# A Householder step with one matmul for both of its row products and one for its update, layer 0's work cut into finer pieces beside it

## The chip, the cores and the metric

The kernel runs on one NeuronCore of one Trainium2 chip. The metric is the device time of one execution in microseconds (us), as the median of several runs. The profile is that of one execution, taken by the hardware profiler.

## The reference, cut to what matters

A stack of four graph layers works on `x` of 128 x 64 x 256 (batch, nodes, features) with one adjacency matrix of 64 x 64. Each layer normalises its input over the features, applies a ReLU, and adds its result to `x`.

```python
h = relu(layernorm(x)); x = x + L0(h, adj)   # A_hat mix, Linear 256->512, batchnorm, relu, Linear 512->256, batchnorm
h = relu(layernorm(x)); x = x + L1(h, adj)   # below
h = relu(layernorm(x)); x = x + L2(h, adj)   # two mixes with Linear, then LSTMs over windows of 1 to 4 nodes
h = relu(layernorm(x)); x = x + L3(h, adj)   # attention over 512 edges

def L1(features, A, W1, b1, W2, b2):
    deg = sum(A, axis=0) + sum(A, axis=1) - diagonal(A)
    d = where(deg > 0, rsqrt(deg), 0)
    L_norm = d[:, None] * (diag(deg) - A) * d[None, :]
    _, U = eigh(L_norm)
    agg = einsum('mn,bnd->bmd', U.T, features)
    return einsum('nm,bmd->bnd', U, relu(agg @ W1 + b1) @ W2 + b2)
```

All is float32. Layer 1 needs the eigenvectors `U` of a symmetric 64 x 64 matrix, which depends on `adj` alone. Layer 0 does not need them.

## The kernel before, in words

The engines are TensorE (PE), VectorE (DVE), ScalarE (ACT), GpSimd (POOL) and SyncE (SP, which issues the DMAs). A TensorE instruction loads a stationary operand ("weights", LDWEIGHTS) and streams a moving one through it (MATMUL); a float32 matmul shows in the trace as two passes, so two of each.

The method `eigenvectors` runs first. It puts two kinds of work on the same engines:

- The eigenvector computation of the class `Fast`: `tridiagonal` turns the matrix into a tridiagonal one in 62 Householder steps (`householder`, for c = 63 down to 2). Then `vectors` finds eigenvalues and vectors and ends in a verdict, a count of failures. Its matmuls write PSUM tiles called `fps` and `fvps`.
- Layer 0. `hidden0` walks over 16 blocks of 512 rows of `x` (tiles `X`): for each one, `hidden_block` normalises, mixes the nodes by a block-diagonal matrix `BDH` and multiplies by the first Linear's weights into four PSUM banks `ps`; ACT copies each bank and DVE takes its batchnorm statistics. When all blocks are through, `features0` applies batchnorm and ReLU and multiplies by the second Linear's weights. Before its first product stand 28 matmuls that only keep TensorE running while the statistics are finished. A product here is `ps<-z,w`.

A planner written out by hand (`Plan`) sets the order. A `chain` step is placed on its engine as soon as what it needs is ready. A `beside` step waits in the engine's queue, as filler: ahead of each chain step, `fill` takes filler that would be done before the chain step can start, or late by no more than the engine's slack. The planner reckons with a busy time and a time until ready for each step, both given in the code.

```python
plan = Plan(dict(T=0.6, S=0.3, V=0.3), 5)      # slack in us: T TensorE, S ScalarE, V VectorE; 5 PSUM banks
...
if at is not None and (at + x.busy <= until + self.slack[engine] or x.urgent and at <= until):
```

After `tridiagonal`, `plan.emit()` emits all planned steps in order of their planned time, and TensorE, VectorE and ScalarE keep that order. `vectors` and what is left of layer 0 (`plan.rest()`) are then emitted in turn and interleaved by the framework's own scheduler. A branch on the verdict follows ("holds"), with a slower eigenvector method for the case of failures, then layers 1 to 3.

One Householder step works on the symmetric matrix `A`, its c-th row `x` copied onto 64 partitions, and these operations:

- TensorE: `zp`, the row c-1 of A on c partitions (a column of the identity as weights), and `yp`, the row c of A likewise; both come from A as it stands after the last update.
- ACT: `s0`, the root of the row's square sum; a copy of one element to `OA`; `z`, the copy of `zp` out of PSUM.
- DVE, on one element in each partition: half the sign (`q`), 1/s0 (`r`), `tt`, `nb` = q tt, the corrected elements of `x`, and `KAP`, the reciprocal.
- DVE: `uA` = z nb + yp. ACT: `uk` = KAP x, and SP stores the row `x` in `V` for later.
- DVE: `c2`, the sum over uA uk / 2 (tile `junk`), then `v` = x c2 - uA.
- TensorE: the update, `uk` times `v` plus `v` times `uk`, two matmuls with one row each that accumulate in one PSUM tile. DVE adds it to A.
- DVE: the next row x in two operations from `uk`, `v` and `z`, without waiting for the update of A. ACT: its square sum (tile `ja`).

All operations of TensorE, DVE and ACT go through a recording helper, so the trace gives them one line, L799 (L800 in the changed kernel); tiles tell them apart.

Of the kernel before, what the change touches and what calls it, by code (L numbers as in the profile page):

```python
# [8 lines left out]
F32 = mybir.dt.float32  # L9
I32 = mybir.dt.int32  # L10
AF = mybir.ActivationFunctionType
ALU = mybir.AluOpType
# [772 lines left out]
GRID = 64  # L785

# [56 lines left out]
class Plan:  # L843
# [55 lines left out]

    def rest(self):  # L900

        while any(self.queue.values()):
            for e in self.queue:
                self.fill(e, 1e9)
# [8 lines left out]
class Fast:  # L913
# [31 lines left out]
    def sum(self, out, a, s, b, op0, op1=ALU.mult, name="junk"):  # L945

        w = a.shape[-1]
        j = self.t(f"{name}{a.shape[0]}", a.shape[0], 64)
        self.o.stt(j[:, 0:w], a, s, b, op0, op1, acc=out)
# [3 lines left out]
    def constants(self):  # L953
# [6 lines left out]
        self.P = t("P", 64, 1)  # L960
        iota(self.P[:], [[0, 1]], 0, 1)
# [21 lines left out]
        o.ts(self.low[:], self.J[:64, :], self.P[:], ALU.is_lt)  # L983
# [3 lines left out]
        o.copy(pi[:], self.P[:])  # L987
# [15 lines left out]
    def tridiagonal(self, S, made, plan):  # L1003
# [3 lines left out]
        A = self.A = t("A", 64, 64)  # L1007
# [3 lines left out]
        for x in (KAP, NB, V):  # L1011
            nc.vector.memset(x[:], 0.0)
        s0, r, tt, q, c2 = (t("h_" + x, 64, 1) for x in "s0 r t q c2".split())
        ja = t("ja", 64, 64)
        bc = lambda c, n=64: c.to_broadcast([n, 64])
        now = {}
        go = plan.chain

        def keep(name, a, b):
            now[name] = self.mm((a, b))  # L1020

        d = go("T", lambda: keep("p", S, self.JR[:]), [made], 0.3, 0.5)
        d = go("V", lambda: o.copy(m[:], now["p"][:]), [d], 0.15, 0.28)
        d = go("T", lambda: keep("p", self.JR[:], m[:]), [d], 0.3, 0.5)
        rest = go("V", lambda: o.copy(A[:], now["p"][:]), [d], 0.15, 0.28)
        d = go("T", lambda: keep("p", bc(ident[:64, 63:64]), A[:]), [rest], 0.3, 0.5)

        def first():
            x = now["x"] = self.rows.tile([64, 65], F32, name="f_x", bufs=8)
            o.copy(x[:, 0:63], now["p"][:, 0:63])  # L1030

        def square(w):
            x = now["x"]
            self.act(ja[:, 0:w], x[:, 0:w], AF.Square, accum_out=x[:, w:w + 1])

        row = go("V", first, [d], 0.15, 0.28)
        h = go("S", lambda: square(63), [row], 0.34, 0.42)
        for c in range(63, 1, -1):
            row, h, rest = self.householder(c, now, go, row, h, rest, (s0, r, tt, q, c2), square)

    def householder(self, c, now, go, row, h, rest, scalars, square):

        o, nc, t = self.o, self.nc, self.t
        ident = self.k.ident
        A, NB, OA, KAP, V = self.A, t("NB", 64, 64), t("OA", 64, 64, 2), t("KAP", 64, 64), t("V", 64, 64)
        s0, r, tt, q, c2 = scalars
        bc = lambda a, n=64: a.to_broadcast([n, 64])
        x = lambda a, b: now["x"][:, a:b]
        nb = NB[:, c - 1:c]
        e, w = 0.001 * c, c - 1  # L1050

        def zy():
            now["zp"] = self.ps.tile([64, 64], F32, name="fps")
            nc.tensor.matmul(now["zp"][:, 0:c], bc(ident[0:c, c - 1:c], c), A[0:c, 0:c], start=True, stop=True)
            now["yp"] = self.ps.tile([64, 64], F32, name="fps")
            nc.tensor.matmul(now["yp"][:, 0:c], bc(A[0:c, c:c + 1], c), A[0:c, 0:c], start=True, stop=True)

        def row_z():
            now["z"] = self.rows.tile([64, 64], F32, name="f_z")
            self.act(now["z"][:, 0:c], now["zp"][:, 0:c], AF.Copy)  # L1060

        def row_uk():

            nc.sync.dma_start(V[c:c + 1, 0:c], now["x"][0:1, 0:c])
            now["uk"] = self.rows.tile([64, 64], F32, name="f_uk")
            self.act(now["uk"][:, 0:c], x(0, c), AF.Copy, scale=KAP[:, c:c + 1])

        def row_uA():
            now["uA"] = self.rows.tile([64, 64], F32, name="f_uA")
            o.stt(now["uA"][:, 0:c], now["z"][:, 0:c], nb, now["yp"][:, 0:c], ALU.mult, ALU.add)  # L1070

        def row_v():
            now["v"] = self.rows.tile([64, 64], F32, name="f_v")
            o.stt(now["v"][:, 0:c], x(0, c), c2[:], now["uA"][:, 0:c], ALU.mult, ALU.subtract)

        def outer():
            uk, v = now["uk"], now["v"]
            p = now["p"] = self.ps.tile([64, 64], F32, name="fps")
            nc.tensor.matmul(p[0:c, 0:c], uk[0:1, 0:c], v[0:1, 0:c], start=True, stop=False)
            nc.tensor.matmul(p[0:c, 0:c], v[0:1, 0:c], uk[0:1, 0:c], start=False, stop=True)  # L1080

        def row_x():
            now["x"] = self.rows.tile([64, 65], F32, name="f_x", bufs=8)
            o.stt(x(0, w), now["uk"][:, 0:w], now["v"][:, w:c], now["z"][:, 0:w], ALU.mult, ALU.add)


        z = go("T", zy, [rest], 0.34, 0.42)
        sq = go("S", lambda: self.act(s0[:], x(c, c + 1), AF.Sqrt), [h], 0.13, 0.23)
        oa = go("S", lambda: self.act(OA[:, c, 1:2], x(c - 1, c), AF.Copy), [row], 0.12, 0.22)
        zs = go("S", row_z, [z], 0.15, 0.26 + e)  # L1090
        sg = go("V", lambda: o.ts(q[:], x(c - 1, c), **halve(0)), [row])
        d = go("V", lambda: o.recip(r[:], s0[:]), [sq])
        d = go("V", lambda: o.stt(tt[:], r[:], x(c, c + 1), s0[:], ALU.mult, ALU.add), [d, h])
        b = go("V", lambda: o.mul(nb, q[:], tt[:]), [d, sg])
        d = go("V", lambda: o.stt(x(c - 1, c + 1), OA[:, c, :], nb, x(c - 1, c + 1), ALU.mult, ALU.add), [b, oa])
        d = go("V", lambda: o.recip(KAP[:, c:c + 1], x(c, c + 1)), [d])
        uk = go("S", row_uk, [d], 0.16, 0.32 + e)
        d = go("V", row_uA, [zs, b, z], 0.12 + e, 0.25 + e)
        d = go("V", lambda: self.sum(c2[:], now["uA"][:, 0:c], 0.5, now["uk"][:, 0:c], ALU.mult), [uk, d],
               0.2 + e, 0.28 + e)  # L1100
        v = go("V", row_v, [d], 0.15 + e, 0.26 + e)
        p = go("T", outer, [v], 0.25, 0.45)
        if c > 2:
            row = go("V", row_x, [v], 0.15 + e, 0.22 + e)
            row = go("V", lambda: o.stt(x(0, w), now["v"][:, 0:w], now["uk"][:, w:c], x(0, w), ALU.mult, ALU.add),
                     [row], 0.15 + e, 0.25 + e)
            h = go("S", lambda: square(w), [row], 0.28 + e, 0.36 + e)
        rest = go("V", lambda: o.add(A[0:c, 0:c], A[0:c, 0:c], now["p"][0:c, 0:c]), [p], 0.12 + e, 0.22 + e)
        return row, h, rest

    def reflectors(self):
# [8 lines left out]
        self.sum(kc[:], self.KAPs[:], 1.0, ident, ALU.mult)  # L1120
# [22 lines left out]
    def scale(self):  # L1143

        o, nc, t = self.o, self.nc, self.t
        NB, A = t("NB", 64, 64), self.A
        self.KAPs = t("KAP", 64, 64)
        DM, NE = t("DM", 64, 64), t("NE", 64, 64)
        o.mul(DM[:], A[:], self.k.ident[:64, :64])
# [316 lines left out]
class Kernel:  # L1466
# [340 lines left out]
    def hidden_block(self, i, r, m, plan, needs, used):  # L1807
# [9 lines left out]
        def mix(dc):  # L1817
            p = now["m", dc] = psum.tile([P, BT], F32, name="ps")
            for j in range(TPB):
                self.mm(p[:, j * P:(j + 1) * P], now["h"][:, j, dc * P:(dc + 1) * P], self.BDH[:])  # L1820
# [966 lines left out]
```

## Time and profile before

| | us |
|---|---|
| median of 3 runs | 2329.3 |
| lowest and highest run | 2326.33, 2331.57 |
| profiled execution: span from first to last instruction | 2325.1 |
| profiled execution: its own time around the span | not recorded apart; the span lies 1.2 under the lowest run |
| start until the first Householder matmul | 11.7 |
| Householder with layer 0 beside it, until its last outer product | 272.1 |
| the rest of the eigenvector work with layer 0, until the verdict's matmul | 364.6 |
| branch | to about 378 |
| layers 1 to 3 | to the end |
| mean granted TensorE clock | 0.997 of full speed |

The span is what the profile can explain; the times of the runs are what a change is judged by. The chain that ended last is followed back from the last instruction; the waits of an engine tell whom it waited for; the timeline gives single instructions with start and duration. The weights for the first product arrive early (the first product starts at 22.5), the first mix runs at 17.3, and layer 0's last product ends at about 364.3, with the verdict's matmul right behind it.

### The profile page before, as it was taken

The page shows a single profiled execution, that of the slowest core. Times are in us where ns is not written, and L with a number is a line of the kernel's source. Part 1 is how long each engine was busy: PE and PEld are TensorE (multiplying, and loading weights), DVE is VectorE, ACT ScalarE, POOL GpSimd, SP SyncE. Part 2 cuts the span into 40 slices and gives each one's busy share as a digit, 9 for nine tenths or more (in the row PEclk, how much of TensorE's full clock was granted, in tenths as well). Part 3 has the DMA queues.
Part 4 walks back from the last instruction along what each step waited for, and adds up shares of the span by engine and source line. Part 5 has one row for each costly group of instructions (what it writes and reads, how often), then busy time and mean ns, then how long its engine had stood idle before and what let it go on. Part 6 is the DMA issues. An engine that isn't in the chain of part 4 may idle for free.

```text
span 2325.1 us, 32725 instructions
## 1 busy us (share of the span) xinstructions
PE 2283.6 (98%) x12169; PEld 1633.1 (70%) x12169; DVE 1629.3 (70%) x4054; ACT 1139.5 (49%) x2483; POOL 3.0 (0%) x26
## 2 busy tenths in 40 slices
PE   7999998999999999999999999999999999999999
PEld 4554445676777788888999998888885544554544
DVE  8887676888447777666767676559756686766667
ACT  5765865754436654433444444336435544444321
POOL 0000000000000000000000000000000000000000
PEclk9999999999999999999999999999999999999999
DMA  5000211230000000001000002000010000000001
GB/s 171 1 1 26 65 56 30 71 83 19 1 37 0 1 19 1 1 1 37 1 1 1 1 1 73 1 1 17 1 46 28 1 5 15 15 19 14 14 24 46
DMA packets 61065, 54.81 MB, mean 24 GB/s; under 512 B 15203, under 2 KB 58724, under 8 KB 60900
## 3 DMA queue, kind: packets, MB, share of 16 engines
q1 hardware_dynamic: 60900, 52.66, 7.4%
q8 instruction: 97, 1.59, 0.3%
q14 instruction: 68, 0.56, 0.1%
HBM read 35.86 MB, written 16.78 MB: 23 GB/s over the span
## 4 chain that ended last, share of the span: by engine, by line
PE 79%; DVE 3%; issue 1%; ACT 1%; DMA 0%; SPq 0%; ACTq 0%; DVEq 0%
PE ps L799 69%; PE acc L799 5%; PE pt L799 4%; PE pe L799 1%; PE y L799 1%; DVE aw L799 1%; DVE X L799 1%; DVE sm_m L799 0%; DVE XV L799 0%; ACT ls_g L799 0%; ACT h L799 0%; DVE ls_g L799 0%; ACT big L799 0%; DVE ls_t L799 0%; DVE sm_e L799 0%
## 5 line engine op out<-in xcount | busy, mean ns | idle before, releaser
L799 ACT ACTIVATE ls_g<-ls_g,ls_b 128x512 f32<-128x512 f32 (+4 forms) x472 | 243.1, 565 | 151.4 <-DVE ls_g L799 149.6
L799 ACT ACTIVATE ls_g<-ps,ls_b 128x256 f32<-128x256 f32 (+3 forms) x268 | 115.5, 470 | 330.9 <-PE ps L799 327.7
L799 PE MATMUL ps<-z,w 128*128 128x512 f32 x512 | 254.9, 621 | 0.9 <-ACT z L799 0.9
L799 PE MATMUL ps<-big,X 128*128 128x176 f32 (+3 forms) x848 | 212.7, 366 | 0.1
L799 DVE TENSOR_TENSOR ls_g<-ls_z,ps 128x512 f32<-128x512 f32 (+5 forms) x256 | 146.8, 579 | 91.9 <-PE ps L799 90.4
L799 DVE TENSOR_TENSOR aw<-at,ed_OST 128x1024 f32<-128x1024 f32 x128 | 149.9, 1219 | 83.0 <-PE ps L799 82.8
L799 PE MATMUL ps<-ls_tx,X 128*128 128x160 f32 (+2 forms) x960 | 206.8, 326 | 0.6 <-ACT ls_g L799 0.6
L799 PE MATMUL ps<-X,X 128*128 128x160 f32 (+1 forms) x896 | 199.1, 306 | 0.0
L799 PE MATMUL ps<-X,ls_w 128*128 128x256 f32 x640 | 190.5, 379 | 0.0
L799 PEld LDWEIGHTS ps<-ls_tx,X 128*128 128x128 f32 x960 | 161.8, 190 | 15.1 <-DVE X L799 4.8
L799 PEld LDWEIGHTS ps<-big,X 128*128 128x128 f32 x848 | 145.9, 190 | 29.7 <-issue 19.4
L799 DVE TENSOR_TENSOR X<-ls_g 128x1024 f32<-128x1024 f32 (+2 forms) x108 | 117.4, 1087 | 49.9 <-ACT ls_g L799 49.8
L799 ACT ACTIVATE r<-ps 128x512 f32<-128x512 f32 x256 | 131.6, 614 | 41.5 <-PE ps L799 41.4
L799 PEld LDWEIGHTS ps<-X,X 128*128 128x128 f32 x896 | 148.4, 190 | 0.0
L799 PE MATMUL ps<-X,ls_s 128*128 128x256 f32 x480 | 142.3, 379 | 0.0
L799 PEld LDWEIGHTS ps<-z,w 128*128 128x128 f32 x512 | 87.2, 190 | 69.0 <-issue 60.2
L799 PE MATMUL ps<-ls_tx,ls_s 128*128 128x256 f32 x464 | 134.8, 379 | 0.0
L799 PE MATMUL ps<-ed_S,Q 64*128 64x512 f32 x512 | 132.9, 618 | 1.4 <-DVE hT L799 0.7
L799 PE MATMUL ps<-ls_tx,ls_w 128*128 128x256 f32 x464 | 133.2, 380 | 0.0
L799 PEld LDWEIGHTS ps<-X,ls_w 128*128 128x128 f32 x640 | 121.4, 190 | 16.8 <-DVE X L799 0.3
L799 PE MATMUL ps<-big,ls_w 128*128 128x256 f32 x464 | 131.9, 379 | 0.7 <-ACT ls_z L799 0.7
L799 PE MATMUL ps<-aw,ed_ODT 128*64 128x512 f32 x512 | 117.3, 595 | 0.1
(545 smaller groups left out, 4019.0 us busy)
## 6 DMA issues: line engine op xcount, KB each, us to landing
X<-in_x_dram SPq DMA_DIRECT2D x32, 512.0 KB
xs<-X SPq DMA_DIRECT2D x16, 512.0 KB
X<-xs SPq DMA_DIRECT2D x16, 512.0 KB
out_dram<-X SPq DMA_DIRECT2D x31, 256.0 KB
X<-in_L_gnn_Wih_t_dram SPq DMA_DIRECT2D x4, 512.0 KB
ls_w<-in_L_gnn_Wih_t_dram SPq DMA_DIRECT2D x4, 512.0 KB
ls_w<-in_L_gnn_Whh_t_dram SPq DMA_DIRECT2D x4, 512.0 KB
w<-in_L_gnn_W_t_dram SPq DMA_DIRECT2D x2, 512.0 KB
```

The source lines that it names most:

```text
L799: i = method(*a, **kw)
```

## The change

- z and y come from one matmul. Its weights `EX` have 128 columns: one half is a unit vector c-1 in each column, written by ACT (`unit`, two steps ahead); the other is the column c of A, masked to its rows, written by DVE (`m`) from the PSUM tile of the update, ahead of the add to A.
- The update is one matmul of "uneven" operands `L` (left) and `R` (right) with 65 rows: rows 0 to 63 of `R` are `v`, of `L` they are zero but for row 0; row 64 of both holds the other vectors. ACT writes the single rows (`side`): minus uA into row 64 of `L`, KAP x into row 0 of `L` and row 64 of `R`. `A` has a 65th row of zeros.
- The scalars: `qh` = q times the square sum (DVE), `qs` = q s0 (ACT), `nb` = r qh + qs (DVE). The sum is over KAP uA x and no longer reads `uk`. The first part of the next row is made from `uk`, `uA` and `z` ahead of the update. The copy into `OA` moves from ACT to POOL; `Plan` gets an engine P for it.
- Layer 0: a mix comes in two halves, a product in halves of 256 columns; each is a filler step of its own. The instructions of a mix stay as they are, those of a product double and halve in size.
- Layouts: `Plan.weigh` lays out each Householder step 27 times, with slacks T of 0.2, 0.45 or 0.8, S of 0.1, 0.3 or 0.6, V of 0.1, 0.35 or 0.65, and keeps the one with the greatest value of busy time by engine (T 1.0, S 0.5, V 2.0) less 2.7 times the end of the step.

```diff
+    def weigh(self, make, slacks, worth, cost):
+        free, queue = dict(self.free), {e: list(v) for e, v in self.queue.items()}
+        n, k = len(self.steps), len(self.opened)
+        best = None
+        for slack in [*slacks, None]:
+            self.slack = slack or best[1]
+            made = make()
+            if slack is None:
+                return made
+            gain = sum(x.busy * worth.get(x.engine, 0.0) for x in self.steps[n:])
+            gain -= cost * max(x.at + x.ready for x in made)
+            if best is None or gain > best[0]:
+                best = gain, slack
+            for x in self.steps[n:]:
+                x.at = None
+            del self.steps[n:], self.opened[k:]
+            self.free, self.queue = dict(free), {e: list(v) for e, v in queue.items()}
...
-        for x in (KAP, NB, V):
+        for x in (A, NB, KAP, V):
             nc.vector.memset(x[:], 0.0)
+        self.left, self.right = ([t(f"{n}{i}", R, 66) for i in range(2)] for n in ("L", "R"))
+        self.ex = [t(f"EX{i}", R, 2, 64) for i in range(2)]
+        for x in (*self.left, *self.right, *self.ex):
+            nc.gpsimd.memset(x[:], 0.0)
+        for c in (63, 62):
+            self.unit(c)
...
+        self.slacks = [dict(T=a, S=b, V=v, P=0.0) for a in (0.2, 0.45, 0.8) for b in (0.1, 0.3, 0.6) for v in (0.1, 0.35, 0.65)]
...
         for c in range(63, 1, -1):
-            row, h, rest = self.householder(c, now, go, row, h, rest, (s0, r, tt, q, c2), square)
+            row, h, rest = plan.weigh(lambda: self.householder(c, now, go, row, h, rest),
+                                      self.slacks, dict(T=1.0, S=0.5, V=2.0), 2.7)
+
+    def unit(self, c):
+        self.act(self.ex[c % 2][0:64, 0, :], self.k.ident[0:64, c - 1:c].to_broadcast([64, 64]), AF.Copy)
...
-        def zy():
-            now["zp"] = self.ps.tile([64, 64], F32, name="fps")
-            nc.tensor.matmul(now["zp"][:, 0:c], bc(ident[0:c, c - 1:c], c), A[0:c, 0:c], start=True, stop=True)
-            now["yp"] = self.ps.tile([64, 64], F32, name="fps")
-            nc.tensor.matmul(now["yp"][:, 0:c], bc(A[0:c, c:c + 1], c), A[0:c, 0:c], start=True, stop=True)
+        def products():
+            zy = now["zy"] = self.ps.tile([P, 64], F32, name="fps")
+            nc.tensor.matmul(zy[:, 0:c], ex[c % 2][:].rearrange("p a b -> p (a b)"), A[:, 0:c], start=True, stop=True)
...
         def outer():
-            uk, v = now["uk"], now["v"]
-            p = now["p"] = self.ps.tile([64, 64], F32, name="fps")
-            nc.tensor.matmul(p[0:c, 0:c], uk[0:1, 0:c], v[0:1, 0:c], start=True, stop=False)
-            nc.tensor.matmul(p[0:c, 0:c], v[0:1, 0:c], uk[0:1, 0:c], start=False, stop=True)
+            p = now["p"] = self.ps.tile([P, 64], F32, name="fps")[:R]
+            nc.tensor.matmul(p[:, 0:c], left[:, 0:R], right[:, 0:c], start=True, stop=True)
...
-        oa = go("S", lambda: self.act(OA[:, c, 1:2], x(c - 1, c), AF.Copy), [row], 0.12, 0.22)
+        oa = go("P", lambda: nc.gpsimd.tensor_copy(OA[:, c, 1:2], x(c - 1, c)), [row], 0.2, 0.4)
...
+        uA = go("V", row_uA, [b, zy, zs], 0.12 + e, 0.25 + e)
+        sides = [go("S", lambda: side(left[64:65, 0:c], now["uA"], -1.0), [uA], 0.14, 0.27 + e)]
+        k = go("V", lambda: o.recip(kap, x(c, c + 1)), [d], 0.09, 0.25)
+        uk = go("S", row_uk, [k], 0.16, 0.32 + e)
+        sides += [go("S", lambda out=out: side(out, now["x", c], KAP[0:1, c:c + 1]), [k], 0.14, 0.27 + e)
+                  for out in (left[0:1, 0:c], right[64:65, 0:c])]
+        d = go("V", lambda: self.sum(dd[:], now["uA"][:, 0:c], kap, x(0, c), ALU.mult), [uA, k], 0.2 + e, 0.28 + e)
+        v = go("V", lambda: o.stt(right[0:64, 0:c], x(0, c), dd[:], now["uA"][:, 0:c], ALU.mult, ALU.subtract),
+               [d], 0.12 + e, 0.26 + e)
         if c > 2:
-            row = go("V", row_x, [v], 0.15 + e, 0.22 + e)
+            row = go("V", row_x1, [uk], 0.12 + e, 0.26 + e)
+        p = go("T", outer, [v] + sides, 0.25, 0.45)
+        if c > 2:
+            row = go("V", lambda: o.stt(nx(0, w), right[0:64, 0:w], now["uk"][:, w:c], nx(0, w), ALU.mult, ALU.subtract),
+                     [row, v], 0.12 + e, 0.25 + e)
+            h = go("S", lambda: self.square(now["x", w], w), [row], 0.28 + e, 0.36 + e)
+            m = go("V", lambda: o.stt(ex[w % 2][0:64, 1, :], now["p"][0:64, w:c].to_broadcast([64, 64]), A[0:64, w:c],
+                                         self.MK[:, w:c].to_broadcast([64, 64]), ALU.add, ALU.mult), [p], 0.12, 0.25)
         rest = go("V", lambda: o.add(A[0:c, 0:c], A[0:c, 0:c], now["p"][0:c, 0:c]), [p], 0.12 + e, 0.22 + e)
+        if c > 3:
+            go("S", lambda: self.unit(c - 2), [zy], 0.14, 0.3)
...
-            plan = Plan(dict(T=0.6, S=0.3, V=0.3), 5)
+            plan = Plan(dict(T=0.6, S=0.3, V=0.3, P=0.0), 5)
...
-            x = beside("T", lambda dc=dc: mix(dc), h, 0.98, 1.1, bank)
+            x = beside("T", lambda dc=dc: mix(dc, 0), h, 0.5, 0.6, bank)
+            x = beside("T", lambda dc=dc: mix(dc, 1), [x], 0.5, 0.66)
...
-            x = beside("T", lambda hc=hc: product(hc, 0), mixed, 0.86, 0.9, bank)
-            x = beside("T", lambda hc=hc: product(hc, 1), [x], 0.86, 1.0)
+            x = beside("T", lambda hc=hc: product(hc, 0, 0), mixed, 0.43, 0.43, bank)
+            for k, kc in ((0, 1), (1, 0), (1, 1)):
+                x = beside("T", lambda hc=hc, k=k, kc=kc: product(hc, k, kc), [x], 0.43, 0.6 if k and kc else 0.43)
...
-                for kc in range(4):
-                    x = beside("T", lambda oc=oc, kc=kc, f=product: f(oc, kc), [z[kc]] + ([x] if x else []), 0.86, 1.0,
-                               None if kc or x else bank)
+                for k in range(2):
+                    for kc in range(4):
+                        x = beside("T", lambda oc=oc, k=k, kc=kc, f=product: f(oc, k, kc), [z[kc]] + ([x] if x else []),
+                                   0.43, 0.6, None if kc or x else bank)
```

## The prediction

> **What bounds the kernel now.** I read the page first, then the busy time by stretch, the waits of TensorE (PE) in the two stretches that the change touches, single PE visits in the timeline, and the weight loads by tile.
>
> The page says that PE is busy from end to end, and that layer 0's products are its costliest group here:
>
> ```profile
> PE 2283.6 (98%) x12169; PEld 1633.1 (70%) x12169; DVE 1629.3 (70%) x4054; ACT 1139.5 (49%) x2483; POOL 3.0 (0%) x26
> ...
> PE 79%; DVE 3%; issue 1%; ACT 1%; DMA 0%; SPq 0%; ACTq 0%; DVEq 0%
> ...
> L799 PE MATMUL ps<-z,w 128*128 128x512 f32 x512 | 254.9, 621 | 0.9 <-ACT z L799 0.9
> ```
>
> Cut at the stages (busy PE, PE weight loads, DVE, ACT, POOL, then the clock): Householder 12 to 272 us, the rest of the eigenvector work to 364.6, the branch to 378.
>
> ```profile
> 11.70:272.10 260.40, 250.58 (x1160) 130.34 (x1160) 195.34 (x1011) 178.88 (x610) 0.00 (x0) 0.99 0.15 44
> 272.10:364.60 92.50, 89.75 (x307) 40.27 (x303) 70.58 (x338) 55.79 (x141) 0.00 (x0) 1.00 0.16 46
> 364.60:378.00 13.40, 7.43 (x51) 7.03 (x51) 6.41 (x32) 4.61 (x10) 0.74 (x3) 0.87 0.32 76
> ```
>
> PE is 96 to 97% busy in both. DVE has 75% and ACT 69%, so neither is full, though each small operation can queue behind a 0.5 to 0.7 us one of layer 0. What PE waited for (total, times, longest), Householder first, then the second stretch:
>
> ```profile
> PE fps L799 <- DVE f_v L799: 3.7, 4, 1.4
> PE fps L799 <- DVE m_m L799: 2.4, 1, 2.4
> PE ps L799 <- ACT z L799: 1.4, 2, 0.9
> PE fps L799 <- DVE f_A L799: 0.9, 2, 0.6
> ...
> PE fps L799 <- DVE f_PB L799: 1.5, 1, 1.5
> PE fps L799 <- DVE f_w_g L799: 1.3, 1, 1.3
> ```
>
> The 62 eigenvector steps hold PE up for some 5 us only (`f_v`, `f_A`); from start to start of its instructions I find 8.9 us beyond the pace it keeps elsewhere. The chain of scalars is hidden: layer 0 fills each gap. One step reads so (start, duration):
>
> ```profile
> 61.33 0.32 PE L799 MATMUL fps<-f_A,ident 53*64 53x53 f32 x2
> 61.48 0.28 PE L799 MATMUL fps<-f_A 53*64 53x53 f32 x2
> 61.69 2.84 PE L799 MATMUL ps<-z,w 128*128 128x512 f32 x6
> 64.46 0.30 PE L799 MATMUL fps<-f_v,f_uk 1*53 1x53 f32 x2
> 64.60 0.26 PE L799 MATMUL fps<-f_uk,f_v 1*53 1x53 f32 x2
> ```
>
> Each matmul is two passes. z and y start 0.15 us apart, six passes of layer 0 follow at 0.43 us, then the outer product. So this stage ends when PE has done a fixed amount of work plus its gaps. A shorter chain is worth nothing unless it closes a gap.
>
> **The change part by part.**
>
> *One matmul for z and y, one for the update.* A visit of PE costs its own passes plus a slower turn into it (0.522 us start to start in place of 0.429) and out of it (0.533). Over all steps the z,y pair takes a mean 0.435 us of PE, the outer pair 0.345 (0.45 at 63 columns down to 0.26 at 2). For the merged z,y the nearest row is a lone 128-column load followed by a short matmul:
>
> ```profile
> 358.94 0.43 PE L799 MATMUL fvps<-U,I 64*128 64x64 f32 x2
> 359.30 1.13 PE L799 MATMUL ps<-z,w 128*128 128x512 f32 x2
> 360.36 0.43 PE L799 MATMUL fvps<-UT,I 64*128 64x64 f32 x2
> ```
>
> That visit is 0.455 at 64 columns and some 0.43 on the mean width; the update, with 65-column weights at every step, some 0.32 (a lone 64-column visit: 0.348 at 64 columns). Gain: 62 x 0.005 + 62 x 0.025, about 1.8 us. It is small because a second matmul inside a visit costs only 0.116 us more: what a visit costs is the turn, and the turns stay. Loads explain it:
>
> ```profile
> L799 PEld LDWEIGHTS fps<-f_A,ident x128: 127/130/228, 11.0 to 273.2; 64*64 64x64 f32 x4, 63*64 63x64 f32 x2, 62*64 62x64 f32 x2, 61*64 61x64 f32 x2
> ...
> L799 PEld LDWEIGHTS fps<-f_v,f_uk x124: 75/103/225, 14.8 to 272.0; 1*63 1x63 f32 x2, 1*62 1x62 f32 x2, 1*61 1x61 f32 x2, 1*60 1x60 f32 x2
> ...
> L799 PEld LDWEIGHTS fvps<-UT,I x2: 183/184/186, 360.4 to 360.5; 64*128 64x128 f32 x2
> ```
>
> The Trainium skill ("TensorE: Matmul & The Clock Gate", "LDWEIGHTS (loading the stationary operand)") says that a load takes columns / 1.2 ns, whatever the rows. By it a 128-column load is two 64-column ones (107 against 53 ns), the merge saves no load time, and the update loads 65 columns where it loaded 2 to 63, 4 x 13 ns less 2 x 1 on the mean: no gain in loads, and about 1 us lost on the update if nothing hid them. The rows here give 130 against 184 ns: a load has a fixed part, so merging two saves about 76 ns per pass pair. I take the trace (-1.8), and keep 0 for the high end.
>
> *Layer 0 in half pieces.* Streaming is unchanged: a 256-column pass takes 0.215 us where the LSTM stage runs it, half of 0.429, with its 0.190 us load hidden below it. 512 more passes cost nothing as long as that load stays hidden. Halves beside a small visit: bounds 0 and 0.05 us each at some 60 places; I take 0, and 3 us for the range.
>
> *The row chain.* Removed: the sum's wait for `uk`, one DVE scalar, `x1`'s wait for `v`. From start to start on DVE and ACT, a step's loop (square, sqrt, reciprocal, ..., next square) takes 3.3 us when nothing is in the way; the new one about 2.6 by the same spacings. The mean PE work of a step is 3.76 us now, so the chain is hidden today and more so afterwards: 0, except through the planner.
>
> *The layouts.* The planner now chooses for each step how much filler goes in, at a price of 2.7 per us of the step's end. In the compiled order of the changed kernel PE gets a mean 3.40 us per step in place of 3.76: filler between z,y and the outer product 117.4 us in place of 136.1, between outer and the next z,y 45.8 in place of 48.8. It is more uneven. Between outer and z,y, 26 steps have one half product only (0.43 us) and 5 none, where before 3 had none (once layer 0 runs) and the others 0.86 or more. Between z,y and outer: 1 none, 5 with 0.43, 9 with about 0.87, against 1 none and 4 with about 0.87. What must fit there:
> - outer, add to A, next z,y: 0.92 us before; 1.03 after, since the new DVE operation `m` goes ahead of the add. With none 0.78 is open (0.66 before), with 0.43 about 0.2.
> - z,y to outer: z 0.36, uA 0.24, sum 0.30, v 0.24, to PE 0.38, in all 1.52 in both. Open: 1.24 with none, 0.62 with 0.43, 0.19 with 0.87.
>
> Gaps after: 5 x 0.78 + 26 x 0.2 + 1.24 + 5 x 0.62 + 9 x 0.19 = 15.1 us. The same sum for before: 3 x 0.66 + 1.24 + 4 x 0.19 = 4.0 of the measured 8.9; the other 4.9 come from operations that queue behind layer 0 on DVE and ACT. With the shorter chain I leave half of that: 17.5. Cost: 17.5 - 8.9 = +8.6 us.
>
> *Single rows on ACT, `OA` on POOL.* ACT gets 248 more operations (sides, unit vectors, `qs`, less `OA`) at 0.093 to 0.11 us of spacing, 26 us in the stage; it goes from 162 to about 169 us of occupancy in a shorter stage, 72%. Not a bound; but the sides and `uk` stand in a row there, and the outer product now waits for both. From `KAP`: 0.19, then three at 0.11, then 0.38 to PE, 0.9 in all, while v takes over 1.0: hidden. If the three fell behind a 0.7 us ReLU, PE would wait 0.6. The 62 POOL copies are in no row of before; nearest is POOL's IOTA of the same tile, 0.131 us. The Trainium skill ("SBUF — State Buffer", "SBUF: two separate sides") calls the port pair of DVE and GpSimd an exclusive lock against a DVE operation with two SBUF inputs; POOL is at 0.00 in these stretches, so no row shows it. By it 62 x 0.13 = 8 us of DVE at worst; without it 0. The copy is needed 1 us after its row is there and its partner is DVE: I take 0, since DVE has slack on most steps.
>
> *Beyond the steps.* Less filler beside Householder leaves 4.3 us less beside the next stretch too (76 products in place of 81) and 26.2 us of layer 0 (61 halves) after its last small matmul, where before there were none. The work on PE is the same, in another place; that tail is full. For the second stretch I add 1.5 us, half of what its filler loses, since its chain is as long as before. The tail after the last product (5.9 us to the first one behind the branch, 370.16) loses 0.3: the branch is decided earlier. The start (six memsets on POOL, three small DVE operations, two unit vectors and a table load of 1.28 on ACT, which idles 4.09 before its first sqrt) lies in front of the first mix at 17.3, which waits for adjacency and X: 0. DMA numbers and SP's order are unchanged.
>
> Sum: -1.8 + 8.6 + 1.5 - 0.3 = +8.0 us on a span of 2325.1, which is 4.2 below the median of the runs, 2329.3 (its own time lies in their 2326.3 to 2331.6 if it is like them). Forecast 2337.
>
> **The rivals.**
> *The gaps close (faster).* If the shorter chain lets a step's z,y and outer be ready early, as a plan that weighs the end of each step intends, then the 8.9 us shrink. At its best: 6 of 8.9 saved, 1.8 by visits, 0.3 tail: 2321. For it: the four `f_v` waits (3.7 us) sit on the path that gets shorter. Against: half of the steps get less filler than their loop through A needs, and that loop grows. It decides if outer to z,y costs under 0.6 us: then 0.43 fills it.
> *PE-bound, nothing moves.* Filler left out comes later on a PE that is full anyway and the gaps are as before; -2 to +3: 2330. For it: PE 96%.
> *ACT and the port lock.* A quarter of the steps wait 0.6 for sides (9 us) and DVE is held 4 us: +20: 2349.
> *The change doesn't do what it says:* on PE it removes 0.03 us per step; included in all.
>
> **How the numbers follow.** Forecast 0.5 (own range 2332 to 2343), faster 0.22, nothing 0.18, ACT and port 0.10. 0.2% is 4.7 us, about what a measurement of this kernel can tell. Of the forecast 0.06 is within it, of "nothing" 0.17: faster 0.23, same 0.23, slower 0.54. The range, 2320 to 2348, takes the faster case nearly whole and leaves the ends out.
>
> **What would show it.** Householder's last outer product at about 250 us in place of 272; the verdict's matmul (`f_k_bad`) 25 us ahead of layer 0's last product, and that one at about 372 in place of 364; PE waits of 15 to 18 us in Householder, most of them on `f_A` or `f_EX`; visits near 0.43 and 0.32; 256-column products at 0.215 per pass. Wrong if those waits stay under 9 us, if the last product comes before 364, or if products beside small visits run slower than 0.215.

## The result, and the profile after

The changed kernel takes 5617.4 us, the median of its runs (5616.5 to 5619.8), against 2330.4 of the kernel before: a ratio of 2.413, 95% interval 2.410 to 2.417. The profiled execution's own time is 5616.5, its span 5614.7.

The profile's page says at once that this is not the loss that was forecast: PE is no longer the engine that bounds the program, and for most of the time its clock is at half.

```profile
PE 2373.4 (42%) x12738; PEld 1785.7 (32%) x12738; DVE 4338.6 (77%) x23282; ACT 1371.0 (24%) x3540; POOL 14.8 (0%) x96
...
PE   7891110000000000000000000099999999999999
...
PEclk9895555555555555555555555599999999999999
```

DVE has 23282 instructions where the kernel before has 4054. They do work that the kernel before never does: behind the branch on the verdict runs the slower eigenvector method. Cut at the stages (columns as before the prediction):

```profile
11.70:301.80 290.10, 236.52 (x1163) 190.45 (x1162) 215.30 (x1072) 226.76 (x815) 10.99 (x62) 0.90 0.11 34
301.80:391.70 89.90, 86.70 (x448) 66.51 (x446) 70.70 (x338) 57.66 (x141) 0.00 (x0) 1.00 0.18 55
391.70:418.50 26.80, 26.72 (x124) 23.20 (x124) 0.15 (x1) 16.02 (x40) 0.00 (x0) 1.00 0.14 42
418.50:3654.00 3235.50, 77.48 (x291) 40.84 (x291) 2685.97 (x19153) 165.61 (x812) 0.26 (x2) 0.50 0.00 0
```

So there are two losses. The fallback takes 3235 us (last row: 19153 DVE instructions of 0.14 us on the mean; the clock column, third from the right, is at 0.50 there). Ahead of it layer 0's last product ends at 418.4 in place of 364.4, 54 us later. The second loss is the one that the prediction was about, and PE's waits in the Householder stretch (total, times, longest) show it:

```profile
PE fps L800 <- DVE f_x L800: 27.2, 25, 2.3
PE fps L800 <- DVE f_h_q L800: 15.7, 22, 1.4
PE fps L800 <- ACT f_R L800: 5.7, 14, 1.3
PE ps L800 <- ACT z L800: 2.8, 6, 1.0
```

Two of these names mislead. `f_x` is put down as what the outer product waits for, and `f_h_q` as what z,y waits for; neither reads them. One step in the timeline of PE, ACT and DVE shows who was last:

```profile
66.98 0.40 PE L800 MATMUL fps<-f_A,f_EX 65*128 65x52 f32 x2 [1.36 <-DVE f_h_q L800]
67.22 0.67 PE L800 MATMUL ps<-BDH,z 128*128 128x128 f32 x4
69.43 0.46 PE L800 MATMUL fps<-f_R,f_L 65*65 65x52 f32 x2 [1.54 <-DVE f_x L800]
69.69 2.04 PE L800 MATMUL ps<-z,w 128*128 128x256 f32 x4
...
68.20 0.24 ACT L800 ACTIVATE f_L<-f_uA 1x52 f32<-1x52 f32 x1
68.47 0.34 ACT L800 ACTIVATE f_uk<-f_x,f_KAP 64x52 f32<-64x52 f32 x1
68.71 0.32 ACT L800 ACTIVATE f_L<-f_x,f_KAP 1x52 f32<-1x52 f32 x1
69.04 0.34 ACT L800 ACTIVATE f_R<-f_x,f_KAP 1x52 f32<-1x52 f32 x1
...
68.58 0.27 DVE L800 SCALAR_TENSOR_TENSOR f_R<-f_x,f_h_d,f_uA 64x52 f32<-64x52 f32 x1
68.84 0.26 DVE L800 SCALAR_TENSOR_TENSOR f_x<-f_uk,f_uA,f_z 64x51 f32<-64x51 f32 x1
69.14 0.27 DVE L800 SCALAR_TENSOR_TENSOR f_x<-f_R,f_uk,f_x 64x51 f32<-64x51 f32 x1
69.93 0.28 DVE L800 SCALAR_TENSOR_TENSOR f_EX<-fps,f_A,f_MK 64x64 f32<-64x64 f32 x1 [0.53 <-PE fps L800]
```

v (`f_R` by DVE) is there at 68.85. ACT's last row, `f_R` from x and KAP, ends at 69.38, and the outer product starts at 69.43. In 46 of the 62 steps it starts less than 0.1 us behind ACT's last row, while v has been ready for a mean 0.59 us. Had ACT's row been early, about 46 x 0.54 = 25 us of waiting would not be there (an estimate from these two figures). `f_x`, the second part of the next row, happens to end at 69.41; in 27 of 61 steps the outer product starts before that part has ended. ACT's four operations, over all steps (min, median, max ns):

```profile
L800 ACT ACTIVATE f_L<-f_uA x62: 201/228/253, 13.5 to 300.5; 1x63 f32<-1x63 f32 x1, 1x62 f32<-1x62 f32 x1, 1x61 f32<-1x61 f32 x1, 1x60 f32<-1x60 f32 x1
...
L800 ACT ACTIVATE f_L<-f_x,f_KAP x62: 278/306/331, 14.0 to 300.9; 1x63 f32<-1x63 f32 x1, 1x62 f32<-1x62 f32 x1, 1x61 f32<-1x61 f32 x1, 1x60 f32<-1x60 f32 x1
...
L800 ACT ACTIVATE f_R<-f_x,f_KAP x62: 292/320/345, 14.4 to 301.2; 1x63 f32<-1x63 f32 x1, 1x62 f32<-1x62 f32 x1, 1x61 f32<-1x61 f32 x1, 1x60 f32<-1x60 f32 x1
...
L800 ACT ACTIVATE f_uk<-f_x,f_KAP x62: 295/322/348, 13.8 to 300.7; 64x63 f32<-64x63 f32 x1, 64x62 f32<-64x62 f32 x1, 64x61 f32<-64x61 f32 x1, 64x60 f32<-64x60 f32 x1
```

From start to start they stand 0.255, 0.228 and 0.319 us apart (medians), and the last is 0.32 long.

The table gives the same stretch for the kernels compared below, from their matmul records: the start of the first mix, the starts of the last outer product and of the verdict's matmul (of each the second pass), the end of layer 0's last product, the time without a matmul in the Householder stretch (from the first mix on) and in the next, and layer 0's PE work beside Householder (0.429 us for each pass of 512 columns, 0.215 of 256, 0.111 of 128).

| kernel | first mix | last outer | verdict | layer 0 ends | idle, Householder | idle, next | layer 0 beside Householder |
|---|---|---|---|---|---|---|---|
| before | 17.3 | 272.0 | 364.4 | 364.4 | 6.8 | 2.8 | 178.6 |
| after | 21.1 | 301.7 | 391.7 | 418.4 | 47.7 | 3.2 | 156.7 |
| e2 guard | 21.1 | 300.5 | 392.2 | 418.9 | 49.3 | 3.2 | 156.7 |
| e3 two matmuls | 20.5 | 275.5 | 367.9 | 389.4 | 16.7 | 3.5 | 161.8 |
| e11 rows on POOL | 21.2 | 286.7 | 376.5 | 403.2 | 36.1 | 3.3 | 156.7 |
| e4 old update | 20.0 | 285.3 | 375.3 | 373.1 | 12.8 | 5.3 | 185.4 |
| e9 old update, full pieces | 20.2 | 281.2 | 372.2 | 359.6 | 11.2 | 12.3 | 190.6 |
| e6 before, pieces | 17.0 | 267.4 | 357.2 | 370.2 | 7.2 | 3.3 | 170.8 |
| e14 before, weighed | 20.9 | 282.7 | 373.5 | 360.9 | 2.1 | 12.3 | 190.6 |
| e15 weighed, 3.5 | 20.2 | 268.0 | 360.3 | 360.3 | 2.8 | 2.7 | 178.6 |

The 54 us of after are then: 3.8 from the later first mix, 40.9 more idle time in Householder, 0.4 more in the next stretch, and by subtraction some 9 of PE work. These 9 are a difference of two larger figures. Ten stretches of Householder, 58 us in all, ran at half the clock (last section); they hold 53 us of PE's work, which at the mean pace of the same passes outside them would have taken 29. So the low clock cost about 24 us. Against it PE needed some 14 us less for the rest, mostly since the merged matmuls came out much cheaper than the prediction had them.

### The profile page after: what moved, and what is told of

Its sections match the earlier page's. It is cut to its first block, busy times and chain, and to the rows that moved or that the text cites. A ratio compares the mean times of both kernels' runs of the same rounds, so it can differ in the third digit from the quotient of the medians.

```text
span 5614.7 us, 56993 instructions
## 1 busy us (share of the span) xinstructions
PE 2373.4 (42%) x12738; PEld 1785.7 (32%) x12738; DVE 4338.6 (77%) x23282; ACT 1371.0 (24%) x3540; POOL 14.8 (0%) x96
## 5 line engine op out<-in xcount | busy, mean ns | idle before, releaser
L457 ACT ACTIVATE e_q_r_y<-e_q_r_hh 64x1 f32<-64x1 f32 x540 | 109.7, 203 | 1357.4 <-DVE e_q_r_hh L51 1234.8
L800 PE MATMUL ps<-z,w 128*128 128x256 f32 x1024 | 273.0, 415 | 2.9 <-ACT z L800 2.0
L800 PEld LDWEIGHTS ps<-z,w 128*128 128x128 f32 x1024 | 198.9, 205 | 32.4 <-ACT z L800 5.7
L68 DVE RECIPROCAL e_q_r_r<-e_q_r_y 64x1 f32<-64x1 f32 x540 | 83.7, 155 | 153.6 <-ACT e_q_r_y L457 150.9
L800 PEld LDWEIGHTS ps<-ls_tx,X 128*128 128x128 f32 x960 | 161.8, 190 | 15.3 <-DVE X L800 4.9
```

Source lines behind the costliest of these rows:

```text
L68: self.v.reciprocal(o, a)
L457: nc.scalar.activation(y[:], hh[:], AF.Sqrt)
L800: i = method(*a, **kw)
```

## The experiments

**The branch, e1 and e2.** Theory: the new arithmetic makes the verdict fail, and nothing else is behind the 3235 us.

```diff
# e1: the verdict is counted and not acted on
-        o.ts(bad[:], ok[:], 1.0, ALU.not_equal)
+        o.ts(bad[:], ok[:], 1.0, ALU.not_equal, 0.0, ALU.mult)
# e2: an exactly zero |g| does not count as the smallest
         o.mabs(g[:], g[:])
+        o.ts(z[:], g[:], 0.0, ALU.is_equal)
+        o.add(g[:], g[:], z[:])
         o.red(gm[:], g[:], ALU.min)
```

> The changed kernel with the count of failures multiplied by zero ahead of the branch: the verdict is computed and not acted on, so the slower eigenvector method never runs and layer 1 takes whatever the fast method gave. Theory A (the verdict fails on the changed step's numbers, and the fallback behind the branch is most of the loss): about 2384 us, that is 2330.4 before plus the 54 us by which layer 0's last product ends later in the trace (418.4 against 364.3). Rival B (something else than the branch makes the program long, such as the clock at 0.706 through the whole kernel): it stays above 5000 us.

> The changed kernel, complete, with two more DVE operations in the twisted factorisation: an entry of |g| that is exactly zero is set to one before the smallest entry is looked for. Theory A1 (on these inputs one eigenvalue's products cancel to an exact zero at the end of the row, which is then taken for the place of the vector; all else of the fast method is sound): the verdict holds, no fallback, about 2385 us. Rival A2 (the step's operands or its precision are wrong in general, many vectors are off): the verdict still fails and the time stays at about 5617 us.

Measured: e1 2379.5 us, ratio 1.022 (1.020 to 1.024); e2 2380.8, ratio 1.022 (1.020 to 1.025). Both as theory A has it. What e1 returns is wrong (relative error 0.047), so the verdict was right: with the change, the fast method did give bad vectors. e2 takes the fast way with two more operations and without any change to the Householder step. The code shows how an exact zero is fatal: `twisted` looks, for each eigenvalue, for the smallest |g| in the row and builds the vector from that place. g is a sum of two ratios less the diagonal; at the ends of the row one of the ratios is the diagonal itself, so if the other one's numerator, a sum of two products, cancels to exactly zero, g is zero there and wins over the true place. That such a zero was taken is shown by e2; that it was this sum which gave it is read from the code and not shown by a run. The uneven update's arithmetic alone does not bring it (e7 below), nor does the rest of the change with the old update (e4).

**ACT's rows, e3, e4, e11 and e8.** The first takes two of the three rows away, by the uneven update as two matmuls of one row; the second takes the third away as well, with the arithmetic of before; e11 has POOL make the two; e8 tells the planner what they take.

```diff
# e3 (with the guard)
-            nc.tensor.matmul(p[:, 0:c], left[:, 0:R], right[:, 0:c], start=True, stop=True)
+            nc.tensor.matmul(p[0:64, 0:c], left[0:1, 0:64], now["uk"][0:1, 0:c], start=True, stop=False)
+            nc.tensor.matmul(p[0:64, 0:c], now["uk"][0:1, 0:64], right[0:1, 0:c], start=False, stop=True)
...
-        sides += [go("S", lambda out=out: side(out, now["x", c], KAP[0:1, c:c + 1]), [k], 0.14, 0.27 + e)
-                  for out in (left[0:1, 0:c], right[64:65, 0:c])]
+        sides.append(uk)
# e4 (without the guard): uk and v as in before
+            nc.tensor.matmul(p[0:64, 0:c], now["uk"][0:1, 0:64], right[0:1, 0:c], start=True, stop=False)
+            nc.tensor.matmul(p[0:64, 0:c], right[0:1, 0:64], now["uk"][0:1, 0:c], start=False, stop=True)
...
-        d = go("V", lambda: self.sum(dd[:], now["uA"][:, 0:c], kap, x(0, c), ALU.mult), [uA, k], 0.2 + e, 0.28 + e)
+        d = go("V", lambda: self.sum(dd[:], now["uA"][:, 0:c], 0.5, now["uk"][:, 0:c], ALU.mult), [uA, uk], 0.2 + e, 0.28 + e)
# e11 (with the guard)
+        sides += [go("P", lambda out=out: nc.gpsimd.tensor_scalar(out, x(0, c)[0:1], KAP[0:1, c:c + 1], None, ALU.mult), [k], 0.2, 0.35)
# e8 (with the guard): planned busy and ready of minus uA 0.27, 0.3; of uk 0.25, 0.4; of the two rows 0.34, 0.42
```

> As the kernel before it (guard in), but the uneven update as two accumulating matmuls of one row each, so that two of ACT's three single rows (KAP x into L and into R) are gone. Theory C (of the 54 us, most is the outer product waiting for ACT's single rows: in some 45 of 62 steps it starts 0.05 us behind the last of them and about 0.55 us later than v alone would let it): 25 us less than the guarded kernel, about 2360 us, with outer products starting behind v. Rival D (the gaps come from the uneven layout, DVE's statistics ahead of the new operation m and too little filler): within 6 us of the guarded kernel.

> The changed kernel, complete, without the guard, with the update of the kernel before (v with half the sum, uk times v plus v times uk, the sum waiting for uk, x1 for v): the arithmetic that rounds differently is taken back, the merged z,y, OA on POOL, the finer pieces and the weighed layouts stay. Theory A1 with the update as the origin of the other rounding: no fallback. By theory C all three single rows of ACT are gone, for one more wait in the chain (0.4 us): 2345 to 2360 us. Rival (the merged z,y is what breaks the numbers): about 5600 us. Rival D: 2380 us.

> The guarded kernel with the two rows scaled by KAP made by POOL in place of ACT. Theory C (their place in ACT's queue, one behind the other after uk, makes the outer product late): near e3, which has no such rows, 2350 to 2360 us, if POOL needs 0.2 to 0.35 us for each as for its copies (0.178). Rival (any third engine's row is as late, or POOL and DVE hold each other up): 2372 us or more.

> The guarded kernel with the planner's prices alone changed, to what the trace shows of ACT's single rows: minus uA 0.27 busy, uk 0.25, the two rows scaled by KAP 0.34 each, ready after 0.30, 0.40 and 0.42. Theory C1 (the rows are only late because the planner put the outer product and its filler as if they took 0.14): filler moves in front of the outer product, 2350 to 2365 us. Rival C2 (the rows lengthen a chain that PE's work no longer covers): 2375 us or more.

Measured: e3 2354.1 (1.011; 1.009 to 1.013), 26.6 us under e2. What PE waits for in its Householder stretch is now:

```profile
PE fps L800 <- DVE f_h_q L800: 12.6, 18, 2.3
PE fps L800 <- ACT f_uk L800: 5.9, 9, 1.5
PE ps L800 <- ACT z L800: 2.1, 6, 0.8
```

The 27.2 of `f_x` are gone with the two rows; idle time falls from 49.3 to 16.7. The 26.6 us are a net gain: the update's visit costs PE 0.54 us in e3 where the merged one costs 0.18 (last section). e4: 2337.2 (1.0035; 1.0025 to 1.0045), 17 us under e3 and 8 under the bottom of what was expected, and without a fallback: the verdict holds with the old update. What the third row costs by itself is not shown, as e4 has another chain and layout too. PE waits only 4 us less in it than in e3; most of the rest goes with the clock, which was at half in one stretch of its Householder steps in place of six, worth some 11 us of PE's work. e11: 2363.1 (1.015; 1.014 to 1.016), 18 us under e2 and 9 over e3. POOL's rows are late too, in fewer steps:

```profile
PE fps L800 <- DVE f_h_q L800: 12.8, 21, 0.8
PE fps L800 <- DVE f_x L800: 10.3, 10, 1.9
PE fps L800 <- POOL f_R L1137: 9.0, 15, 2.4
```

e8: 2377.4 (1.021; 1.019 to 1.024), C2: a planner that knows the price does not get rid of it. As C2 has it, the rows lengthen a loop (A to z,y to uA to the rows to the outer product to A) that layer 0's work in a step no longer covers.

**The uneven form in the kernel before, e7.** The edit:

```diff
-            nc.tensor.matmul(p[0:c, 0:c], v[0:1, 0:c], uk[0:1, 0:c], start=False, stop=True)
+            nc.tensor.matmul(p[0:c, 0:c], now["nA"][0:1, 0:c], uk[0:1, 0:c], start=False, stop=True)
...
-            o.stt(x(0, w), now["uk"][:, 0:w], now["v"][:, w:c], now["z"][:, 0:w], ALU.mult, ALU.add)
+            o.stt(x(0, w), now["uk"][:, 0:w], now["uA"][:, w:c], now["z"][:, 0:w], ALU.mult, ALU.subtract)
...
+        na = go("S", row_nA, [d], 0.14, 0.27 + e)      # minus uA, one row, on ACT
-        d = go("V", lambda: self.sum(c2[:], now["uA"][:, 0:c], 0.5, now["uk"][:, 0:c], ALU.mult), [uk, d],
+        d = go("V", lambda: self.sum(c2[:], now["uA"][:, 0:c], KAP[:, c:c + 1], x(0, c), ALU.mult), [d],
...
-        p = go("T", outer, [v], 0.25, 0.45)
+        p = go("T", outer, [v, na, uk], 0.25, 0.45)
```

> The kernel before, complete and without a guard, with the uneven update's arithmetic alone: the sum over KAP uA x without waiting for uk, v with the whole sum, uk times v less uA times uk as two matmuls of one row, one more single row on ACT (minus uA). Theory A1 (the exact zero was a matter of which way the roundings fell, not of the uneven form): it may hold, then 2326 to 2336 us, the waiting of the sum for uk gone against one ACT operation of 0.24 us. Rival A3 (the uneven form itself spoils the numbers): fallback, about 5570 us.

Measured: 2355.1 (1.011; 1.009 to 1.014). The verdict holds, so the uneven arithmetic does not spoil the numbers by itself: theory A1, and a fail on one set of roundings of one input. The time lies some 20 us above what was expected. With the sum no longer waiting for `uk`, the planner believed in a shorter step and put 128.7 us of layer 0 beside Householder (178.6 in before); the steps did not get that short, PE was idle for 24.3 us, and 51.5 us of layer 0 came behind the verdict. A chain that is shorter on paper cost time here, as it took cover away; that it was this, and not ACT's added row, is read from the table's figures and not tested by a run of its own.

**Layouts and pieces, e5, e6, e9, e10, e12, e13.**

```diff
# e5 (with the guard), and e10, e12: one layout, slacks 0.6, 0.3, 0.3
-            row, h, rest = plan.weigh(lambda: self.householder(c, now, go, row, h, rest),
-                                      self.slacks, dict(T=1.0, S=0.5, V=2.0), 2.7)
+            row, h, rest = self.householder(c, now, go, row, h, rest)
# e6: the kernel before with hidden_block and features0 of after; e9, e10, e12, e13: e4 with those of before
# e12, e13: the copy to OA on ACT
-        oa = go("P", lambda: nc.gpsimd.tensor_copy(OA[:, c, 1:2], x(c - 1, c)), [row], 0.2, 0.4)
+        oa = go("S", lambda: self.act(OA[:, c, 1:2], x(c - 1, c), AF.Copy), [row], 0.12, 0.22)
```

> The guarded kernel with the weighing of layouts taken out: every Householder step is laid out once, with the slacks of the kernel before (0.6, 0.3, 0.3). Theory C (ACT's single rows are the loss, whatever the layout): within 8 us of the guarded kernel's 2380.8. Rival D (the weighed layouts put too little filler, or DVE's statistics, in the wrong places): 2362 us or less.

> The kernel before with layer 0's finer pieces alone. As the prediction has it the pieces stream as fast as the full ones: within 4 us of the kernel before, either way. Rival E (512 more products, many of them next to a small visit, cost 0.05 us or more each place): 3 to 10 us slower.

> As e4 (the changed kernel with the update of before), but layer 0's mixes and products in full pieces again. The finer pieces alone cost before 4.2 us (e6). If that is a price per piece, this one comes 4 us under e4's 2337.2: 2333. If the finer pieces were what lets e4's layouts fill its gaps, it comes out at 2340 or more.

> As e9 with every step laid out once, with the slacks of before: what is left of the change is the merged z,y with its unit vectors, the scalars with qs on ACT, and OA on POOL. The prediction's -0.4 us for the merged z,y (62 x 0.005) and nothing for the rest: 2326 to 2331 us, as before. Rival (unit vectors, qs and the operation m ahead of the add to A open gaps): 2335 us or more. If it is under 2324, it beats both kernels.

> As e10 with the copy to OA on ACT again, so that POOL does nothing in the steps. If POOL's 62 copies hold DVE up (62 x 0.18 = 11 us at most), this one is faster by some us; if not, the same within 2 us, since ACT is not the bound.

> As e9 (merged z,y, scalars and weighed layouts of the change, update and full pieces of before), with the copy to OA on ACT again. If OA on POOL costs here what it cost between e10 and e12 (5.9 us), this one is at 2326 to 2328, level with before, and the rest of the change is worth nothing either way. If that difference was only one layout against another, it stays at 2331 to 2336 us.

Measured, with the ratio to before: e5 2383.7 (1.024; 1.022 to 1.027): without the weighing the loss is of the same size, theory C. e6 2333.0 (1.0018; 1.0011 to 1.0025): the finer pieces cost some 4 us by themselves, though each streams at 0.215 us; its PE was idle hardly longer than before's (table), so they cost PE work (342.6 us without waits, against 337.6). e9 2332.8 (1.0023; 1.0012 to 1.0033) lies where a price per piece would have it, though its layout differs from e4's and the two intervals overlap. e10 2339.3 (1.0053; 1.0040 to 1.0066) and e12 2333.4 (1.0029; 1.0018 to 1.0040): 6 us less with the copy on ACT, but not by waits (14.4 us idle in e10's Householder stretch, 16.0 in e12's); e10 had more passes at half the clock. And e13 2336.1 (1.0035; 1.0021 to 1.0049), with the copy on ACT, is not under e9, where it is on POOL. So POOL's copies have no cost that these runs can show; each took 0.177 to 0.179 us in after.

**Weighing alone, e14, e15, e16.** The kernel before with `weigh`, at its price of 2.7 for a us of the step's end, then 3.5 and 4.0.

```diff
-            row, h, rest = self.householder(c, now, go, row, h, rest, (s0, r, tt, q, c2), square)
+            row, h, rest = plan.weigh(lambda: self.householder(c, now, go, row, h, rest, (s0, r, tt, q, c2), square),
+                                      slacks, dict(T=1.0, S=0.5, V=2.0), 2.7)      # e15: 3.5, e16: 4.0
```

> The kernel before with the weighed layouts alone. If weighing each step is worth something by itself, 2316 to 2323 us: it can take at most the 6.8 us that PE stands idle in the Householder stretch of before. If the planner's prices are too far from the trace for that (it does not know the 0.5 to 0.7 us behind which small operations queue), 2325 to 2335 us.

> As e14 (the kernel before with weighed layouts), at a price of 3.5 in place of 2.7 for a us of the step's end. Theory F (e14 lost because weighing put 190.6 us of layer 0's PE work beside Householder where before has 178.6, so the second stretch had 12 us too little and PE stood idle 12.3 us there, while its idle time in Householder fell from 6.8 to 2.1): this price puts 178.6 us there, so the second stretch is covered again and some of the 4.7 us stays: 2320 to 2327 us. Rival (weighed layouts are slower for themselves): 2330 us or more.

> As e15 at a price of 4.0, which puts 170.8 us of layer 0 beside Householder, less than before. By theory F the second stretch is covered and a tail of layer 0 follows the verdict, with PE full in it: no slower than before but for idle time in Householder, 2323 to 2332 us. Rival: 2335 us or more.

Measured: e14 2335.0 (1.0028; 1.0019 to 1.0036). Weighing did close gaps: idle time in Householder 2.1 in place of 6.8. It put 12 us more of layer 0 there, and these were missed in the next stretch:

```profile
359.75 1.12 PE L799 MATMUL ps<-z,w 128*128 128x512 f32 x2
366.77 0.31 PE L799 MATMUL fps<-ident,f_w_zs 64*64 64x64 f32 x1 [5.89 <-DVE f_w_zs L799]
...
373.41 0.37 PE L799 MATMUL fps<-f_k_bad,ones 64*64 64x1 f32 x2 [1.98 <-DVE f_k_bad L799]
```

Layer 0 is done at 360.9 and the eigenvector chain goes on by itself to 373.5. At a price of 3.5, e15, both end together at 360.3: 2323.1 us, ratio 0.9976 (0.9965 to 0.9987), some 6 us faster than the kernel before, and the only run here that is faster. At 4.0, e16 2331.2 (1.0006; 0.9998 to 1.0014): a tail of layer 0 follows the verdict. The weighing is worth these 6 us only where its price shares layer 0 out rightly between the two stretches.

## Why the prediction was wrong, point by point

- **The step that failed first** is not in the sum: it took for granted that the branch "is decided earlier", not that it may be decided otherwise. The rivals include no case of another outcome. The update rounds differently, the verdict depends on it, and 3235 us stand behind it; to ask what the branch tests, and what the change does to its inputs, would have made this a case of its own.
- **"then three at 0.11"**: the term for ACT's rows. The spacing of 0.093 to 0.11 was that of operations without a scale from memory. The row for `uk` before (0.35 us for 63 columns) was the nearest one and was not used. Measured 0.23 to 0.32 apart, so the rows end 0.5 us behind v, and "hidden" became 27 us for two of them (e3).
- **"With the shorter chain I leave half of that: 17.5"**: idle time in the Householder stretch was 47.7 us. That the gaps open was right, and so was the place; some 25 of the difference are ACT's rows, which come after v. What the sum had nothing for is that waits so close together also cost clock: about 24 us more.
- **Which gaps**: z,y did wait where `m` stands ahead of the add to A (15.7 us in 22 waits), as named. In 12 of 61 steps `m` started over 1.2 us behind the start of the outer product, held up by layer 0's statistics in 5 and by the next row's second part in 7; the sum reckoned with 0.1 for it.
- **"The start ... 0"**: the first mix came 3.8 us later, and 2.5 us or more later in most of the kernels run. In after the ReLUs that the mix needs start at 20.48 in place of 16.69: in ACT's order they stand behind the second and third step's rows.
- **"Halves ... I take 0, and 3 us for the range"**: about 4 (e6), at the edge of that.
- **"What a visit costs is the turn, and the turns stay", -1.8**: they did not stay. With z and y merged PE needs some 10 us less (328.4 us without waits in e9, 338.1 in e14, which weighs at the same price), though e9's update costs more than e14's; the sum has 62 x 0.005 = 0.3. Where PE waits for nothing, the update's visit sets layer 0 back by 0.18 us in after and by 0.44 in before (last section). The prediction took the merged z,y's cost from a load of 64 rows; the new one has 65. The gain went into waits: PE was idle for 11.2 us in e9's Householder stretch and for 2.1 in e14's. The loads have about the size that the sum used: 0.137 us at 65 columns.
- **POOL's copies "0"**: no run contradicts it (e10 and e12 against e9 and e13). The lock that the prediction weighed is not shown by any.
- **The verdict "25 us ahead of layer 0's last product"**: 26.7. "Householder's last outer product at about 250": 301.7, wrong by the rows.
- Without the branch and the rows, e4 is at 2337.2, the number forecast; as it has the old update (which loads 64 columns at every step, 0.54 us a visit in place of before's 0.44) and another layout, that is luck in the number and not a proof of the sum.

## What to carry to other kernels

Ask of each change that touches numbers which branch reads them, what lies behind it, and with what margin it is decided. When an engine is given small operations on the chain, price them by the nearest operation of the same form, a scale from memory included, and in their order on that engine. Do the same for a small matmul, rows and columns of its weights included. A planner that trades filler against the end of a step must know what the stage after it needs: here 12 us of filler moved from one stretch into the other turned a gain into a loss.

## What the runs showed of the hardware

A row of one partition costs ACT as much as 64 partitions: 0.306 to 0.320 us against 0.322 (median) with a scale from memory, and 0.228 with a constant one.

**The turn into a small matmul depends on the size of its weights.** In e9 the merged z,y (65 rows, 128 columns) and the old update (1 row, 64 columns) stand among the same passes:

```profile
112.73 2.82 PE L800 MATMUL ps<-z,w 128*128 128x512 f32 x6
115.48 0.31 PE L800 MATMUL fps<-f_R,f_uk 1*64 1x43 f32 x2
115.62 0.28 PE L800 MATMUL fps<-f_uk,f_R 1*64 1x43 f32 x2
115.83 1.12 PE L800 MATMUL ps<-z,w 128*128 128x512 f32 x2
116.79 0.31 PE L800 MATMUL fps<-f_A,f_EX 65*128 65x42 f32 x2
116.94 1.96 PE L800 MATMUL ps<-z,w 128*128 128x512 f32 x4
```

How much a visit sets layer 0 back is the time from the start of the pass ahead of it to the start of the second pass behind it, less two passes; here are medians over the visits without a wait at the full clock. In e9 it is 0.23 us for z,y (48 visits) and 0.54 for the update (33); in before 0.54 for z,y (49) and 0.44 for the update (40); in after 0.23 (17) and 0.18 (12). The pass ahead of z,y in e9 takes no longer than any other, and the one ahead of the update 0.09 us longer. In after, visits that begin with 64 rows or fewer, or with 64 columns or fewer, pay these 0.09 us as well; only weights of more than 64 rows and more than 64 columns do not. Why it is so, no run shows.

**The clock went by windows of 3.41 us, and a window that was only half busy lost it.** The 0.90 of after's Householder stretch is the mean of two states: ten stretches of 3.41 to 10.24 us at half, the rest at full. Cut at the ends of such windows (first PE's busy time; third from the right the clock):

```profile
61.70:65.11 3.41, 3.41 (x22) 3.09 (x22) 2.49 (x14) 1.95 (x6) 0.00 (x0) 1.00 0.01 2
65.11:68.52 3.41, 1.42 (x11) 1.06 (x9) 3.00 (x14) 2.64 (x11) 0.18 (x1) 1.00 0.00 0
68.52:71.93 3.41, 2.50 (x9) 2.14 (x9) 2.00 (x12) 2.69 (x10) 0.18 (x1) 0.50 0.01 2
71.93:75.35 3.42, 3.42 (x9) 2.72 (x9) 1.87 (x8) 2.92 (x8) 0.00 (x0) 0.50 0.00 0
75.35:78.76 3.41, 3.41 (x19) 2.92 (x18) 2.45 (x13) 2.28 (x9) 0.18 (x1) 1.00 0.02 5
```

Behind a window with 1.42 us of work the clock is at half, and it comes back behind the first window that is busy throughout. All ten stretches go so: ahead of each stands a window that was 27 to 64% busy, with no wait over 2.1 us in it, and behind its last, full one the clock returns. Of the windows at full clock that were not followed by a drop, the least busy was 58%. Four passes of 256 columns took 2.04 us at half clock (at 69.69 above), and 1.22 at full:

```profile
24.81 1.22 PE L800 MATMUL ps<-z,w 128*128 128x256 f32 x4
```

The Trainium skill ("TensorE: Matmul & The Clock Gate", "Part 1: The HAM clock gate (the "warmup" mystery)") describes a clock that drops to half after an idle window of about 3.4 us. The length of the window agrees, and so does the 0.50 of the fallback, where PE has 77 us of work in 3235; but by idle windows alone the Householder steps, whose longest wait is 2.3 us, would have kept the full clock, and they lost it ten times.
